# A decoder layer on one core: cross attention's outputs turned in 32x32 blocks on VectorE, its steps dealt out anew, and three shared groups in source order behind it

## The chip, the core and the metric

The kernel runs on 1 core of a Trainium2 chip. The metric is device time in microseconds (us), with the median of several runs. Engines are named as in the profile: PE is TensorE's matmul side and PEld its weight loads, DVE is VectorE, ACT is ScalarE, POOL is GpSimd, SP is SyncE, which here only issues DMAs.

## What is computed

One decoder layer over x of 32 batches x 128 tokens x 512 columns, in float32. Three parts follow one another, each on the layer-normalised sum so far and added to it:

```python
x1 = x + self_attention(layernorm(x))        # differential, 16 heads, causal
x2 = x1 + cross_attention(layernorm(x1), c)  # 8 heads of 16 channels
h3 = layernorm(x2)
out = x2 + shared_mlp(h3) + sum(w_k * expert_k(h3) for k in top6)
```

Cross attention works on each batch as a matrix of 128 channels (partitions) by 512 positions. Queries and keys get a rotary turn, a head's softmax runs over all 512 key positions, and a 128x128 matrix `Wo` leads out. The router takes sigmoid scores of 32 experts in four groups, keeps two groups and picks six experts per token. `shared_mlp` is `down(silu(gate) * up)` with 704 hidden columns over every token. An expert is the same with 352, on the tokens that chose it.

## The kernel before

The program is a list of stages on one core. PSUM is one ring of four tiles of two banks each (`Common.banks`): every user of PSUM takes the next tile and waits until its former user is done with it.

*Cross attention* (about 865 to 2058 us) is written as a hand-made software pipeline, `CrossAttention.advance`. One step is one (batch, side, chunk of 128 queries, pair of heads); 16 steps make a batch and are called a period. In step n the kernel issues

- `maxima` of step n: two matmuls (L621) give scores into a PSUM tile, and one VectorE reduce (L625) takes the row maxima, which frees the tile;
- `exponentials` of step n - 11: two matmuls (L644) on scores less maxima, then one ScalarE exponential (L648);
- in the steps that hold one, a `weigh`, in two halves ahead of and behind these (L659): the weighted values and, by a column of ones, the sums of the weights, 128 x 512 in one bank for each side of a batch;
- whatever `plan` has put down for this step: `sooner` calls ahead of maxima, `later` calls behind exponentials.

`plan` gives each operation of a batch its step by a number written out by hand: the projections, rotations (L590 to L598, VectorE and GpSimd), values, turning the maxima, and behind the weighing `divide` (L667), `turn_out` (L685), `leave` (L694), `measure_out`, `normalize_out`, `hand_over`, `router`, and then the routing: `groups` (L880), `choose` (L904), `take` (L923), `count` (L935), `slots_of`, and six `enter` scatters to a table in DRAM (L957). On PE, VectorE, ScalarE and GpSimd the queue order is the source order (`manual_schedule`). Each engine runs its queue in order, so the plan decides what waits behind what.

Divide and turn before: `weigh` copies its result from PSUM to SBUF on ScalarE (L665). `divide` turns it by eight PE transposes (L674), takes the reciprocal of the sums (L677) and multiplies (L680, twice 128x256) out of PSUM. `turn_out` turns it back by four PE transposes (L83) and a ScalarE copy (L688). `leave` (L697) multiplies by `Wo` and adds x1.

*Behind it*, the shared MLP works in eight groups of 4 batches, `Shared.group`: gate and up in five full chunks (L1126), the ends (L1140), a VectorE multiply by the silu of ScalarE (L1132), then down (L1158 and L1164) for two pairs of batches. Each group loads its tokens (`s_hT`). Two groups come early, behind cross attention: the first with pieces of the routing that are left over (`between`, six calls of `cross.rest(16)`, then `routing.tiles`, which finds out which expert each tile of 128 tokens has), the second beside the start of the experts. Here the scheduler, not the source, orders the instructions. The constructor of `Experts` fetches the tables (GpSimd gathers), turns them on PE (L1224, L1234) and computes places; `begin` starts gathers of tokens (L1310) and the weights' DMAs.

*The experts* (2212 to about 3748) run 208 tiles of 128 tokens in source order: gate and up (L1335), down (L1371), and a scatter-add into `sum_d` (L1376). *The tail* is the six other shared groups, whose sums are written to the output; two DMAs copy the finished early batches.

## Time and profile before

| what | us |
|---|---|
| median of 3 runs (lowest to highest) | 4100.53 (4096.46 to 4104.73) |
| the profiled execution, its own time | 4099.66 |
| its span, first to last instruction | 4098.0 |
| mean granted TensorE clock | 0.992 |
| cross attention, one period | 37.14 |
| end of cross attention to the experts' first matmul | 153.6 |
| one shared group in the tail | 57.46 |

The groups of instructions that matter here, from 1000 to 1900 us of the span, in the form line, engine, operation, operands, count, then busy us, mean ns, and the idle time of the engine just ahead of them:

```profile
L621 PE MATMUL ps<-xk,xq 32*128 32x512 f32 x1550 | 428.4, 633 | 0.0
L644 PE MATMUL ps<-xqn,xk 32*128 32x512 f32 x1550 | 418.0, 638 | 0.0
L659 PE MATMUL ps<-xp,v 128*32 128x512 f32 x1552 | 186.6, 598 | 0.0
...
L674 PE MATMUL ps<-ident,xu 128*128 128x128 f32 x192 | 26.2, 279 | 0.0
```

```profile
L625 DVE TENSOR_REDUCE nm<-ps 128x2 f32<-128x1024 f32 x388 | 473.2, 1225 | 149.3 <-PE ps L621 105.5 <-PE ps L644 40.7
```

L621 and L644 use other row groups of the array (32 of the 128 rows) and run side by side, so their busy times overlap, and busy PE is not PE at its peak. The reduces alone fill 473 of 900 us on VectorE.

### The profile page before, as it was taken

What the parts mean: (1) busy time and instruction counts of PE and PEld (TensorE: products, weight loads), DVE (VectorE), ACT (ScalarE), POOL (GpSimd) and SP (SyncE); (2) the same over time, 40 slices, a digit from 0 to 9 for tenths busy, and PEclk for the clock granted to TensorE, in tenths of its full rate; (3) what the DMA queues carried; (4) which work ended last, traced back from release to release, by engine and by line L of the source; (5) the groups of instructions that cost most, each with busy time, mean ns of one, the idle gap of its engine ahead of it and who ended that gap; (6) DMA issues with size and microseconds to landing.
All of it is one profiled execution on the core that took longest, in us unless ns stands there. A gap on an engine that the chain in (4) does not pass through costs nothing. (4 is left out here: it accounts for less than half of the span.)

```text
span 4098.0 us, 59001 instructions
## 1 busy us (share of the span) xinstructions
PE 3979.2 (97%) x20404; PEld 2081.9 (51%) x20404; DVE 2192.4 (54%) x3461; ACT 1245.6 (30%) x1791; POOL 2241.5 (55%) x2420
## 2 busy tenths in 40 slices
PE   7999999989999999999979999999999999999999
PEld 5666666533344444434335555555555555554444
DVE  5777777777888888888722333333333333332111
ACT  3333333235555555555510111111111111111000
POOL 3444444443555555555444777777777777772000
PEclk9999999999999999999999999999999999999999
DMA  3111110021111111111134777686777776774110
GB/s 105 32 32 31 32 32 27 32 80 38 46 45 40 45 45 45 42 42 45 32 125 117 173 171 195 139 198 155 175 158 174 167 182 155 179 179 115 52 62 31
DMA packets 282785, 386.24 MB, mean 94 GB/s; under 512 B 147792, under 2 KB 175056, under 8 KB 282448
## 3 DMA queue, kind: packets, MB, share of 16 engines
q0 software_dynamic: 62912, 109.85, 15.0%
q1 hardware_dynamic: 77680, 186.52, 14.0%
q10 hardware_dynamic: 141888, 86.01, 7.6%
q8 instruction: 165, 2.70, 0.3%
q14 instruction: 140, 1.15, 0.1%
HBM read 616.47 MB, written 142.02 MB: 185 GB/s over the span
## 5 line engine op out<-in xcount | busy, mean ns | idle before, releaser
L1310 POOL DMA_INDIRECT e_xr<-h_d,e_run_of x832 | 849.4, 1021 | 296.3 <-issue 246.8
L625 DVE TENSOR_REDUCE nm<-ps 128x2 f32<-128x1024 f32 x512 | 623.2, 1224 | 199.6 <-PE ps L621 131.4
L648 ACT ACTIVATE xp<-ps 128x1024 f32<-128x1024 f32 x512 | 516.8, 1023 | 432.0 <-PE ps L644 430.3
L1340 DVE TENSOR_TENSOR e_gu<-e_act,ps 128x352 f32<-128x352 f32 x208 | 108.4, 521 | 956.4 <-ACT e_act L1339 956.4
L1371 PE MATMUL ps<-wd,e_guT 128*128 128x512 f32 (+1 forms) x1248 | 571.7, 594 | 2.2 <-issue 2.1
L621 PE MATMUL ps<-xk,xq 32*128 32x512 f32 x2048 | 564.3, 635 | 6.7 <-DVE xres L403 4.3
L644 PE MATMUL ps<-xqn,xk 32*128 32x512 f32 x2048 | 548.1, 638 | 0.6 <-DVE xqn L633 0.6
L1335 PE MATMUL ps<-wg,e_xT 128*128 128x352 f32 x1664 | 527.7, 459 | 4.2 <-DMA wg<-in_L_ffn_w_gate_dram 3.4
L1335 PE MATMUL ps<-wu,e_xT 128*128 128x352 f32 x1664 | 527.1, 460 | 2.0 <-DMA wu<-in_L_ffn_w_up_dram 1.9
L1335 PEld LDWEIGHTS ps<-wg,e_xT 128*128 128x128 f32 x1664 | 314.8, 189 | 238.3 <-issue 103.4
L1335 PEld LDWEIGHTS ps<-wu,e_xT 128*128 128x128 f32 x1664 | 316.4, 190 | 179.7 <-DMA wu<-in_L_ffn_w_up_dram 3.7
L1376 POOL DMA_INDIRECT sum_d<-e_y,e_into x208 | 338.3, 1627 | 116.7 <-issue 65.0
L1339 ACT ACTIVATE e_act<-ps 128x352 f32<-128x352 f32 x208 | 96.3, 463 | 892.8 <-PE ps L1335 818.4
L1371 PEld LDWEIGHTS ps<-wd,e_guT 128*128 128x128 f32 (+1 forms) x1248 | 238.0, 191 | 247.5 <-issue 204.1
L1375 ACT ACTIVATE e_y<-ps,e_weight 128x512 f32<-128x512 f32 x208 | 142.9, 687 | 421.6 <-PE ps L1371 407.2
L621 PEld LDWEIGHTS ps<-xk,xq 32*128 32x128 f32 x2048 | 158.6, 183 | 220.6 <-ACT xp L648 100.4
L957 POOL DMA_INDIRECT table_d<-entry,at x192 | 196.6, 1024 | 108.7 <-DMA table_d<-entry,at 55.0
L1361 DVE STREAM_TRANSPOSE e_guT<-e_gr 96x384 f32<-96x384 f32 (+1 forms) x416 | 230.3, 554 | 37.9 <-DMA e_gr<-e_gu_d 30.6
L659 PE MATMUL ps<-xp,v 128*32 128x512 f32 x2048 | 247.1, 598 | 3.0 <-ACT xp L648 2.6
L1322 DVE STREAM_TRANSPOSE e_xT<-e_xr 128x512 f32<-128x512 f32 x208 | 226.7, 1090 | 6.4 <-DMA e_xr<-h_d,e_run_of 6.4
L239 POOL TENSOR_SCALAR k<-kz,a_keep,a_extra 128x256 f32<-128x256 f32 x128 | 69.8, 555 | 252.4 <-ACT kz L238 252.4
L644 PEld LDWEIGHTS ps<-xqn,xk 32*128 32x128 f32 x2048 | 152.8, 183 | 37.6 <-DVE nm L625 25.6
(265 smaller groups left out, 5071.9 us busy)
## 6 DMA issues: line engine op xcount, KB each, us to landing
wg<-in_L_ffn_w_gate_dram SPq DMA_DIRECT2D x208, 704.0 KB
wu<-in_L_ffn_w_up_dram SPq DMA_DIRECT2D x208, 704.0 KB
wd<-in_L_ffn_w_down_dram SPq DMA_DIRECT2D x208, 576.0 KB
e_gu_d<-e_gu ACTq DMA_DIRECT2D x208, 192.0 KB
e_gr<-e_gu_d ACTq DMA_DIRECT2D x208, 192.0 KB
wd<-in_L_ffn_w_down_dram SPq DMA_DIRECT2D x208, 128.0 KB
e_xr<-h_d,e_run_of POOLq DMA_INDIRECT x832
xin<-in_x_dram SPq DMA_DIRECT2D x32, 256.0 KB
```

The lines of the kernel that those rows point to most:

```text
L621: self.nc.tensor.matmul(sc[:, i, :], q[rows, ts(c, P)], k[rows, :], start=True, stop=True)
L625: self.nc.vector.tensor_reduce(at[:, self.ROW[side], 2 * pair : 2 * pair + 2], sc, AX.X, ALU.max, negate=True)
L644: self.nc.tensor.matmul(sc[:, i, :], k[rows, ts(c, P)], q[rows, :], start=True, stop=True)
L648: self.nc.scalar.activation(e, sc, AF.Exp)
L659: self.nc.tensor.matmul(po[b, side][ts(j, 32), :], self.v2[b % 2][:, c, 2 * j + side, :], es[j // 2][:, j % 2, :], start=c == 0, stop=c == ...
L957: self.nc.gpsimd.indirect_dma_start(out=self.table_ds[k % 2][:, :], out_offset=bass.IndirectOffsetOnAxis(ap=self.at[b][:, k : k + 1], axis=0),
L1310: self.cm.nc.gpsimd.indirect_dma_start(out=xr[:, t, :], out_offset=None, in_=self.h3_d.rearrange("t (q f) -> (t q) f", q=self.Q), in_offse ...
L1322: self.cm.nc.vector.transpose(xT.rearrange("p c (t i) -> p c t i", t=self.Q), self.xr.pop(i).rearrange("p t (j c) -> p c t j", c=EC),)
L1335: nc.tensor.matmul(pgu[:, half, 0:M], t[:, c, :], w[:, c, :], start=c == 0, stop=c == EC - 1)
L1361: self.cm.nc.vector.transpose(t[rows, 0:n, :].rearrange("p c (t i) -> p c t i", t=self.Q), g[rows, :, 0 : 32 * n].rearrange("p t (j c) -> ...
L1371: nc.tensor.matmul(py, t[:n, c, :], self.wd[s][:n, c, :], start=c == 0, stop=c == len(M_CHUNKS) - 1)
L1376: nc.gpsimd.indirect_dma_start(out=self.sum_d[:, :], out_offset=bass.IndirectOffsetOnAxis(ap=self.into[:, i : i + 1], axis=0), in_=y[:, :] ...
```

## The change

- `weigh`: each side's result is turned in 32x32 blocks by a VectorE `transpose` from PSUM straight to SBUF, in place of ScalarE's copy. Both sides go into one tile `xu` of one buffer.
- `divide`: no PE transposes. One reciprocal and one multiply of 128x512 work on `xu` in SBUF.
- `turn_out`: one VectorE `transpose` of 128x512, SBUF to SBUF, in place of four PE transposes and a copy.
- `plan`: `measure` one step earlier, `measure_out` and `normalize_out` two earlier, `sigmoid` split off from `groups` (steps 43 and 46 in place of 45 for both), `choose` and `take` two later, `count` one later, `slots_of` and the scatters two later. At step 480 the tokens of the first shared group are loaded.
- Behind cross attention: three early groups in place of two, in source order on PE, VectorE, ScalarE and GpSimd. The first two carry the rest of the routing in 33 pieces of two steps and `tiles`; the third carries the experts' table work, cut into `fetch`, `arrange`, `turn_tables`, `places` and `first_tokens`, with fixed places. A group's `sum_d` rows are loaded at its start. The tail has five groups, and the last copies cover 12 batches.

```diff
         if half:
-            self.out[b, side] = self.p2.tile([P, E], F32, name="xu")
-            self.nc.scalar.copy(self.out[b, side], po.pop((b, side)))
+            if side == 0:
+                self.out[b] = self.p2.tile([P, 2, E // 32, 32], F32, name="xu", bufs=1)
+            self.nc.vector.transpose(
+                self.out[b][:, side].rearrange("p k r -> p (k r)"), po.pop((b, side))
+            )
 
     def divide(self, b):
 
-        nc, TC, Q, C, out = self.nc, self.TC, self.Q, self.C, self.out
-        tr = self.cm.banks()
-        for side in range(2):
-            u = out.pop((b, side))
-            for c in range(TC):
-                nc.tensor.transpose(tr[:, side, ts(c, P)], u[:, ts(c, P)], self.cm.ident)
-        tr = tr.rearrange("p s (x r) -> p s x r", r=2 * C)
-        rs = self.p2.tile([P, 2, TC * Q], F32, name="xrs")
-        nc.vector.reciprocal(rs, tr[:, :, :, C])
-        out[b] = self.p2.tile([P, TC * Q, 2, C], F32, name="xo")
-        for side in range(2):
-            nc.vector.tensor_tensor(
-                out[b][:, :, side, :], tr[:, side, :, 0:C],
-                rs[:, side].unsqueeze(2).broadcast_to([P, TC * Q, C]), ALU.mult,
-            )
+        nc, C = self.nc, self.C
+        u, n = self.out.pop(b), E // 32
+        rs = self.p2.tile([P, 2, n], F32, name="xrs")
+        nc.vector.reciprocal(rs, u[:, :, :, C])
+        self.out[b] = self.p2.tile([P, n, 2, C], F32, name="xo")
+        nc.vector.tensor_tensor(
+            self.out[b].rearrange("p k s c -> p s k c"), u[:, :, :, 0:C],
+            rs.unsqueeze(3).broadcast_to([P, 2, n, C]), ALU.mult,
+        )
 
     def turn_out(self, b):
-        tr = self.cm.turn4(self.out.pop(b).rearrange("p x s c -> p (x s c)"))
-        self.out[b] = self.p2.tile([P, self.TC, P], F32, name="xoT")
-        self.nc.scalar.copy(self.out[b], tr)
+        o = self.out.pop(b)
+        self.out[b] = self.p2.tile([P, E], F32, name="xoT")
+        self.nc.vector.transpose(self.out[b], o.rearrange("p k s c -> p (k s c)"))
...
-            sooner.put(at + 29, self.measure_out, b)
-            later.put(at + 31, self.normalize_out, b)
+            sooner.put(at + 27, self.measure_out, b)
+            later.put(at + 29, self.normalize_out, b)
             later.put(at + 38, self.hand_over, b)
             later.put(at + 40, self.router, b)
-            later.put(at + 45, routing.groups, b)
-            sooner.put(at + 53, routing.choose, b)
-            later.put(at + 53, routing.take, b)
-            later.put(at + 55, routing.count, b)
-            sooner.put(at + 61, routing.slots_of, b)
+            later.put(at + 43, routing.sigmoid, b)
+            later.put(at + 46, routing.groups, b)
+            sooner.put(at + 55, routing.choose, b)
+            later.put(at + 55, routing.take, b)
+            later.put(at + 56, routing.count, b)
+            sooner.put(at + 63, routing.slots_of, b)
             for k in range(TOPK):
-                later.put(at + 63 + 5 * k // 2, routing.enter, b, k)
+                later.put(at + 65 + 5 * k // 2, routing.enter, b, k)
         later.put(20, load_shared)
+        later.put(2 * S * (self.B - 2), load_tokens)
         for b in range(self.B):
-            sooner.put(2 * S * b - 11, self.measure, b)
+            sooner.put(2 * S * b - 12, self.measure, b)
...
-        todo = [lambda: cross.rest(16)] * 6 + [
+        todo = [lambda: cross.rest(2)] * 33 + [
             lambda: routing.tiles(eid, fresh, rows, used, usual),
             lambda: nc.sync.dma_start(out=sum_d[T : T + P, :], in_=rest),
         ]
...
-        EARLY = 2
-        shared.group(0, False, between)
+        EARLY = 3
+        with tc.manual_schedule(engines=in_order):
+            for g in range(EARLY - 1):
+                shared.group(g, False, between)
+            while todo:
+                between()
+    e_ctx = ctx.enter_context(ExitStack())
+    with tc.manual_schedule(engines=in_order):
+        experts = Experts(
+            cm, e_ctx, table_ds, h3_d, sum_d, w_gate, w_up, w_down, eid, fresh, rows, n_tiles
+        )
+
+        shared.load_rows(EARLY - 1)
+        experts.begin(0, usual)
+        experts.fetch()
+        nothing = lambda: None
+        todo += [nothing] * 3 + [
+            lambda: experts.arrange(0),
+            lambda: experts.arrange(1),
+            nothing,
+            experts.turn_tables,
+            experts.places,
+            experts.first_tokens,
+        ]
+        shared.group(EARLY - 1, False, between)
         while todo:
             between()
-    e_ctx = ctx.enter_context(ExitStack())
-    experts = Experts(
-        cm, e_ctx, table_ds, h3_d, sum_d, w_gate, w_up, w_down, eid, fresh, rows, n_tiles
-    )
-    experts.begin(0, usual)
-    for g in range(1, EARLY):
-        shared.group(g, False)
     experts.run()
```

More of the change, by code (lines that the diff above doesn't have):

```diff
@@ L697, in leave @@
         self.nc.tensor.matmul(
-            py, self.wT["o"], self.out.pop(b).rearrange("p t x -> p (t x)"), start=True, stop=True
+            py, self.wT["o"], self.out.pop(b), start=True, stop=True
         )
@@ L727, in router, with plan @@
         self.routing.scores(b, pl)
-    def plan(self, load_shared):
+    def plan(self, load_shared, load_tokens):
         S, later, sooner, routing = self.S, self.later, self.sooner, self.routing
@@ L878, in scores, with sigmoid @@
         nc.scalar.activation(s, s, AF.Exp)
-    def groups(self, b):
-        nc = self.nc
-        s = self.score.pop(b)
+    def sigmoid(self, b):
+        nc, s = self.nc, self.score[b]
         nc.vector.tensor_scalar(s, s, 1.0, None, ALU.add)
@@ L889, in groups @@
         )
+    def groups(self, b):
+        nc, s, best = self.nc, self.score.pop(b), self.best[b % 2]
         top = self.small("g_top", [P, 8])
@@ L1098, with __init__, use @@
     G = 4
-    def __init__(self, cm, pool, w, h3T_d, sum_d, out):
-        self.cm, self.pool, self.w, self.h3T_d, self.sum_d, self.out = cm, pool, w, h3T_d, sum_d, out
+    def __init__(self, cm, h_pool, h3T_d, sum_d, out):
+        self.cm, self.h_pool, self.h3T_d, self.sum_d, self.out = cm, h_pool, h3T_d, sum_d, out
         self.NB = h3T_d.shape[0]
-        self.hTs = {}
+        self.hTs, self.x2s = {}, {}
+    def use(self, pool, w):
+        self.pool, self.w = pool, w
     def load(self, g):
@@ L1107, in load @@
         if g * G < self.NB and g not in self.hTs:
-            self.hTs[g] = self.pool.tile([P, G, EC, P], F32, name="s_hT", bufs=2)
+            self.hTs[g] = self.h_pool.tile([P, G, EC, P], F32, name="s_hT")
             self.cm.nc.sync.dma_start(
@@ L1111, in load, with rows_of, load_rows @@
             )
+    def rows_of(self, g, pair):
+        b = g * self.G + 2 * pair
+        return self.sum_d[ts(b // 2, 2 * P), :].rearrange("(b p) e -> p b e", p=P)
+    def load_rows(self, g):
+        if g not in self.x2s:
+            self.x2s[g] = []
+            for pair in range(self.G // 2):
+                x2 = self.pool.tile([P, 2, E], F32, name="s_x2", bufs=2)
+                self.cm.nc.sync.dma_start(out=x2, in_=self.rows_of(g, pair))
+                self.x2s[g].append(x2)
     def group(self, g, final, between=lambda: None):
@@ L1118, in group @@
         self.load(g)
+        self.load_rows(g)
         self.load(g + 1)
@@ L1129, in group @@
                     )
+                if i == 0:
+                    between()
             act = pool.tile([P, G, P], F32, name="s_act", bufs=2)
@@ L1151, in group @@
             b = g * G + 2 * pair
-            rows = self.sum_d[ts(b // 2, 2 * P), :].rearrange("(b p) e -> p b e", p=P)
-            x2 = pool.tile([P, 2, E], F32, name="s_x2", bufs=2)
-            nc.sync.dma_start(out=x2, in_=rows)
+            x2 = self.x2s[g][pair]
             py = cm.banks()
@@ L1161, in group @@
                     )
+                between()
             for i in range(2):
@@ L1168, in group @@
             nc.vector.tensor_tensor(x2, x2, py, ALU.add)
-            to = self.out[b : b + 2].rearrange("b p e -> p b e") if final else rows
+            to = (
+                self.out[b : b + 2].rearrange("b p e -> p b e") if final else self.rows_of(g, pair)
+            )
             nc.sync.dma_start(out=to, in_=x2)
-        between()
 class Experts:
@@ L1203, in __init__, with fetch @@
         T = h3_d.shape[0]
-        self.T = T
-        NT = rows.shape[1]
-        entry = cm.banks().rearrange("p o (j t) -> p o j t", j=EC)
-        parts = cm.banks().rearrange("p o (t j x) -> p (o t) j x", t=2, j=2)
-        for j in range(NT):
-            got = [
-                self.p2.tile([P, E], F32, name="e_y")[:, 0 : 2 * P].rearrange("p (s o) -> p s o", o=2)
-                for i in range(len(table_ds))
+        self.T, self.cp, self.rows, self.table_ds = T, cp, rows, table_ds
+        self.NT = rows.shape[1]
+        self.wg = [cp.tile([P, EC, M], F32, name=f"wg{s}") for s in range(SETS)]
+        self.wu = [cp.tile([P, EC, M], F32, name=f"wu{s}") for s in range(SETS)]
+        self.wd = [cp.tile([P, len(M_CHUNKS), E], F32, name=f"wd{s}") for s in range(SETS)]
+        self.gu_s = cp.tile([P, self.Q * self.RUN], F32, name="e_gu")
+        self.row_i = cp.tile([P, 2], I32, name="e_row_i")
+        self.row = cp.tile([P, 2], F32, name="e_row")
+        self.last, self.expert = None, {}
+        self.got, self.spread = {}, {}
+        self.xr, self.xT, self.gu, self.gr, self.guT = {}, {}, {}, {}, {}
+    def fetch(self):
+        nc = self.cm.nc
+        for j in range(self.NT):
+            self.got[j] = [
+                self.p2.tile([P, E], F32, name=("e_y", "e_xT")[j % 2])[:, 0 : 2 * P].rearrange(
+                    "p (s o) -> p s o", o=2
+                )
+                for i in range(len(self.table_ds))
             ]
-            for t, table_d in zip(got, table_ds):
+            for t, table_d in zip(self.got[j], self.table_ds):
                 nc.gpsimd.indirect_dma_start(
@@ L1218, in __init__ @@
                     in_=table_d.rearrange("(n s) o -> n (s o)", s=P),
-                    in_offset=bass.IndirectOffsetOnAxis(ap=rows[:, j : j + 1], axis=0),
+                    in_offset=bass.IndirectOffsetOnAxis(ap=self.rows[:, j : j + 1], axis=0),
                     bounds_check=table_d.shape[0] // P - 1,
                 )
-            nc.vector.tensor_tensor(got[0], got[0], got[1], ALU.add)
-            for o in range(2):
-                nc.tensor.transpose(entry[:, o, j, :], got[0][:, :, o], cm.ident)
@@ L1226, in __init__ @@
-            runs = self.p2.tile([P, self.Q, self.Q, 32], F32, name="e_xr", bufs=3)
-            slots = got[0][:, :, 0].rearrange("p (b t a) -> p t a b", b=self.Q, t=self.Q)
-            for t in range(self.Q):
-                nc.vector.tensor_copy(
-                    runs[:, t].rearrange("p q (a b) -> p q a b", b=self.Q),
-                    slots[:, t].unsqueeze(1).broadcast_to([P, self.Q, 32 // self.Q, self.Q]),
-                )
+        nc.gpsimd.memset(self.gu_s, 0.0)
+        nc.gpsimd.iota(self.row_i, pattern=[[0, 2]], base=self.T + 1, channel_multiplier=1)
@@ new lines, in arrange @@
+    def arrange(self, j):
+        nc = self.cm.nc
+        got = self.got[j]
+        nc.vector.tensor_tensor(got[0], got[0], got[1], ALU.add)
+        runs = self.spread[j] = self.p2.tile([P, self.Q, self.Q, 32], F32, name="e_xr", bufs=3)
+        slots = got[0][:, :, 0].rearrange("p (b t a) -> p t a b", b=self.Q, t=self.Q)
+        for t in range(self.Q):
+            nc.vector.tensor_copy(
+                runs[:, t].rearrange("p q (a b) -> p q a b", b=self.Q),
+                slots[:, t].unsqueeze(1).broadcast_to([P, self.Q, 32 // self.Q, self.Q]),
+            )
@@ L1233, in __init__, with turn_tables @@
+    def turn_tables(self):
+        nc, cm = self.cm.nc, self.cm
+        self.entry_ps = cm.banks().rearrange("p o (j t) -> p o j t", j=EC)
+        self.parts_ps = cm.banks().rearrange("p o (t j x) -> p (o t) j x", t=2, j=2)
+        for j in range(self.NT):
+            got, runs = self.got.pop(j), self.spread.pop(j)
+            for o in range(2):
+                nc.tensor.transpose(self.entry_ps[:, o, j, :], got[0][:, :, o], cm.ident)
             for t in range(self.Q):
                 nc.tensor.transpose(
-                    parts[:, t, j, :], runs[:, t].rearrange("p q i -> p (q i)"), cm.ident
+                    self.parts_ps[:, t, j, :], runs[:, t].rearrange("p q i -> p (q i)"), cm.ident
@@ L1236, in __init__, with places @@
                 )
-        entry = entry.rearrange("p o j t -> p o (j t)")[:, :, 0:n_tiles]
+    def places(self):
+        nc, cp, T, n_tiles = self.cm.nc, self.cp, self.T, self.n_tiles
+        entry = self.entry_ps.rearrange("p o j t -> p o (j t)")[:, :, 0:n_tiles]
         self.weight = cp.tile([P, n_tiles], F32, name="e_weight")
         nc.vector.tensor_copy(self.weight, entry[:, 1, :])
-        row_i = cp.tile([P, 2], I32, name="e_row_i")
-        nc.gpsimd.iota(row_i, pattern=[[0, 2]], base=T + 1, channel_multiplier=1)
+        row_i, row = self.row_i, self.row
@@ L1243, in __init__ @@
         nc.vector.tensor_scalar(row_i[:, 1:2], row_i[:, 1:2], -T - 1, None, ALU.add)
         nc.vector.tensor_scalar(row_i[:, 1:2], row_i[:, 1:2], 5, None, ALU.logical_shift_right)
-        row = cp.tile([P, 2], F32, name="e_row")
         nc.vector.tensor_copy(row, row_i)
+        self.run_of = cp.tile([P, self.Q, self.NT * P], I32, name="e_run_of")
+        nc.vector.tensor_scalar(
+            self.run_of, self.parts_ps.rearrange("p t j x -> p t (j x)"), float(self.Q),
+            float(-self.Q), ALU.mult, ALU.add,
+        )
@@ L1247, in __init__ @@
+        nc.vector.tensor_scalar(self.run_of, self.run_of, 0.0, row[:, 1:2], ALU.max, ALU.add)
         none = cp.tile([P, n_tiles], F32, name="e_none")
@@ L1250, in __init__ @@
         nc.vector.scalar_tensor_tensor(self.into, entry[:, 0, :], -1.0, none, ALU.add, ALU.add)
-        self.run_of = cp.tile([P, self.Q, NT * P], I32, name="e_run_of")
-        nc.vector.tensor_scalar(
-            self.run_of, parts.rearrange("p t j x -> p t (j x)"), float(self.Q), float(-self.Q),
-            ALU.mult, ALU.add,
-        )
-        nc.vector.tensor_scalar(self.run_of, self.run_of, 0.0, row[:, 1:2], ALU.max, ALU.add)
-        self.wg = [cp.tile([P, EC, M], F32, name=f"wg{s}") for s in range(SETS)]
-        self.wu = [cp.tile([P, EC, M], F32, name=f"wu{s}") for s in range(SETS)]
-        self.wd = [cp.tile([P, len(M_CHUNKS), E], F32, name=f"wd{s}") for s in range(SETS)]
-        self.gu_s = cp.tile([P, self.Q * self.RUN], F32, name="e_gu")
-        nc.gpsimd.memset(self.gu_s, 0.0)
-        self.last, self.expert = None, {}
-        self.xr, self.xT, self.gu, self.gr, self.guT = {}, {}, {}, {}, {}
     def weights_in(self, i):
@@ L1387, in begin @@
         self.first, self.end, self.last = first, end, None
-        for i in range(first, first + 3):
-            self.tokens(i)
         for i in range(first, first + SETS):
@@ L1392, in begin, with first_tokens @@
             self.weights_out(i)
+    def first_tokens(self):
+        for i in range(self.first, self.first + 3):
+            self.tokens(i)
     def run(self):
@@ L1454, in decoder_kernel @@
         cross = CrossAttention(cm, x_w, x1_d, x2_d, h3_d, h3T_d, ctx_in, routing)
-        cross.plan(lambda: s_w.load())
+        cross.plan(lambda: s_w.load(), lambda: shared.load(0))
         x_ctx = ExitStack()
@@ L1480, in decoder_kernel @@
         s_w = SharedWeights(cm, s_w_pool, sw_gate, sw_up, sw_down)
+        s_h_pool = ctx.enter_context(tc.tile_pool(name="s_h", bufs=2, reuse_waits="tile"))
+        shared = Shared(cm, s_h_pool, h3T_d, sum_d, out)
         p2 = ctx.enter_context(tc.tile_pool(name="x_p2", bufs=2, reuse_waits="tile"))
@@ L1484, in decoder_kernel @@
         s_pool = ctx.enter_context(tc.tile_pool(name="s_p", bufs=1, reuse_waits="tile"))
-        shared = Shared(cm, s_pool, s_w, h3T_d, sum_d, out)
-        todo = [lambda: cross.rest(16)] * 6 + [
+        shared.use(s_pool, s_w)
+        en = mybir.EngineType
+        in_order = {en.PE, en.DVE, en.Activation, en.Pool}
+        todo = [lambda: cross.rest(2)] * 33 + [
             lambda: routing.tiles(eid, fresh, rows, used, usual),
@@ L1495, in between @@
                 todo.pop(0)()
-        EARLY = 2
-        shared.group(0, False, between)
+        EARLY = 3
[3 more added lines that the diff above has]
+            while todo:
+                between()
+    e_ctx = ctx.enter_context(ExitStack())
+    with tc.manual_schedule(engines=in_order):
+        experts = Experts(
+            cm, e_ctx, table_ds, h3_d, sum_d, w_gate, w_up, w_down, eid, fresh, rows, n_tiles
+        )
+        shared.load_rows(EARLY - 1)
[11 more added lines that the diff above has]
+        shared.group(EARLY - 1, False, between)
         while todo:
             between()
-    e_ctx = ctx.enter_context(ExitStack())
-    experts = Experts(
-        cm, e_ctx, table_ds, h3_d, sum_d, w_gate, w_up, w_down, eid, fresh, rows, n_tiles
-    )
-    experts.begin(0, usual)
-    for g in range(1, EARLY):
-        shared.group(g, False)
     experts.run()
@@ L1513, in decoder_kernel @@
         experts.begin(usual, n_tiles)
+        experts.first_tokens()
         experts.run()
```

## The prediction, made before the result

> **What bounds the kernel now.** I read the page's busy shares and slices first, then the busy time of each engine by stage, then the order of events on PE and VectorE in one cross attention period, then PE's row through the transition.

> ```profile
> PE 3979.2 (97%) x20404; PEld 2081.9 (51%) x20404; DVE 2192.4 (54%) x3461; ACT 1245.6 (30%) x1791; POOL 2241.5 (55%) x2420
> ...
> PE   7999999989999999999979999999999999999999
> PEld 5666666533344444434335555555555555554444
> DVE  5777777777888888888722333333333333332111
> ```

> PE is busy nearly everywhere, VectorE is at 8 tenths in the slices of cross attention and low behind them. The slice in which PE dips to 7 is the transition to the experts. By stage (columns: window, length, then PE, PEld, DVE, ACT, POOL busy, clock, DMA):

> ```profile
> 1000.00:1900.00 900.00, 884.67 (x5860) 363.46 (x5862) 728.06 (x1191) 529.57 (x653) 503.69 (x720) 1.00 0.14 44
> ...
> 2058.30:2211.90 153.60, 131.30 (x350) 62.28 (x350) 34.36 (x103) 17.40 (x26) 54.78 (x74) 0.93 0.40 127
> ```

> Cross attention looks bound by PE (98%), yet this hides a wait. One period (one batch, 16 steps) takes 37.14 us: the first matmul of L580 for x-rows comes at 1525.15 and again at 1562.29. PE's pieces laid end to end make about 33.7: 16 steps of 1.07, four weigh halves of 1.86, and the projections, turns, divide, leave, hand-over, count and router. In a step the maxima matmuls (L621) and the exponentials' (L644) run side by side, and when one of the pair is held back PE still counts as busy. What holds them shows at the divide:

> ```profile
> 1515.15 1.09 PE L674 MATMUL ps<-ident,xu 128*128 128x128 f32 x8
> ...
> 1517.57 0.63 PE L83 MATMUL ps<-ident,xo 128*128 128x128 f32 x4 [0.19 <-DVE xo L680]
> 1518.12 0.70 PE L621 MATMUL ps<-xk,xq 32*128 32x512 f32 x2
> 1518.63 0.70 PE L644 MATMUL ps<-xqn,xk 32*128 32x512 f32 x2
> ```

> ```profile
> 1514.97 1.23 DVE L625 TENSOR_REDUCE nm<-ps 128x2 f32<-128x1024 f32 x1 [0.93 <-PE ps L621]
> 1516.28 0.36 DVE L677 RECIPROCAL xrs<-ps 128x32 f32<-128x32 f32 x1
> 1516.67 0.75 DVE L680 TENSOR_TENSOR xo<-ps,xrs 128x256 f32<-128x256 f32 x2
> 1517.34 1.23 DVE L625 TENSOR_REDUCE nm<-ps 128x2 f32<-128x1024 f32 x1
> ```

> The reduce that began at 1517.34 ends at 1518.57 and L644 starts at 1518.63: the exponentials wait for the PSUM tile (a ring of four) that VectorE's reduce frees, not for PE. The loop is: maxima start, +1.17 reduce starts, +1.23 ends, +0.05 exponentials start, 2.45 us in all, against 1.07 for a step on PE alone. So cross attention is bound by the queue order of VectorE as much as by PE. I rebuilt a period from this rule and the queue orders, and it gave the starts of before to 0.05 us; I use the same walk for after.

> **The change in cross attention.** Per batch PE loses 8 transposes of L674 (1.02 us) and 4 of L83 (0.55), with 0.19 of idle before them: 1.76. ScalarE loses two copies of 0.585 (L665) and one of 0.580 (L688): 1.75. VectorE keeps the reciprocal (0.36), trades two multiplies (0.75 together) for one of 512 elements, and gains three block transposes. The nearest rows (min/median/max ns):

> ```profile
> L386 DVE STREAM_TRANSPOSE anT<-an x32: 694/698/711, 90.2 to 869.8; 128x512 f32<-128x512 f32 x32
> L352 DVE TENSOR_TENSOR o<-u,rs x64: 668/693/1528, 75.4 to 859.9; 128x512 f32<-128x512 f32 x64
> L928 DVE TENSOR_TENSOR hits<-number,picked x32: 346/1334/1368, 1010.4 to 2101.0; 128x192 f32<-128x192 f32 x32
> ```

> From PSUM L339 turns 128x768 in 974 ns; between 0.70 (as L386, and 974 scaled by size is 0.65) and 0.98 I take 0.70. VectorE per batch: 3 x 0.70 + 0.36 + 0.68 - 1.11 = +2.0, on 30.1 now (728.06/900 of 37.14).

> [...] The trace agrees for L928: 0.35 alone, 1.33 usually, as at 1530.38 to 1531.73, where GpSimd's L592 ran until 1531.50. If the divide behaves as alone it costs 0.68[...]. By the new queue order GpSimd has only the groups' small operations then (0.19 to 0.71), so I take 0.68 and keep 1.9 for the range. [...]

> Walking the new order through the loop, in three stretches that change (the rest of the period stays):

> - From step 15's maxima to the end of the k projection (L580): 12.42 before (1513.79 to 1526.21). Transposes and two PSUM tiles are gone, but reduce, reciprocal, multiply, reduce, turn, reduce now stand in one chain on VectorE: from step 15's maxima 1.17 + 1.14 + 0.39 + 0.60 + 1.14 + 0.61 + 1.23 + 0.05 = 6.33 to step 2's exponentials (pitches, slightly under durations). Result 11.94: -0.48 where PE alone would give -1.76.
> - From the weigh of step 5 to the router's end: 10.95 before (1526.21 to 1537.16). `choose` and `take` stand at step 7 now, `count` at 8; count's matmul (L940) waits for `taken` (L933) behind two reduces. Reduce 6 ends at 7.18, choose 0.72, reduce 7 to 9.04, L928 0.36 and L933 0.49: taken at 9.83, while PE is done at 9.15. Result 11.45: +0.50. I take L928 at 0.36, since the rotation's GpSimd work, which blocked it at step 5, is over by then; blocked, it adds 1.0. If PE has other work in hand, this stretch gives 0.
> - From the q projection to the weigh of step 13: 1.32 before. The row statistics of the output (1.01 on VectorE) now stand before reduce 11 and so before the exponentials: 1.95, +0.63. Unless the order has slack, then 0.

> Moved steps bring their DMAs and GpSimd calls along: six scatters per batch two steps later, the h3 stores as before, and one 1 MB load of tokens at step 480 on SP, where the queue is nearly empty (DMA share 0.14). I cost these at nothing; the cover is GpSimd at 56% here. The sum is +0.6 us a period, with bounds -0.1 (second and third stretch hidden) and +1.9 (divide blocked). Some 28 full periods: +17. The end of the stage gains 2.57 of wait (below): cross attention +15.

> **The transition.** From the end of cross attention to the experts it takes 153.6 now, with two shared groups. PE waits:

> ```profile
> 2057.21 1.05 PE L659 MATMUL ps<-xp,v 128*32 128x512 f32 x4 [2.57 <-ACT xp L648]
> 2062.50 5.53 PE L1126 MATMUL ps<-s_hT,sg 128*128 128x512 f32 x8 [4.23 <-DMA s_hT<-h3T_d]
> ...
> 2130.54 7.38 PE L1158 MATMUL ps<-sd,s_gu 128*128 128x512 f32 x12 [7.25 <-DVE s_gu L1132]
> ```

> With the smaller ones between them (1.33, 0.68, 0.31, 2.80, 3.34, 2.40) they make 24.9, and the mean clock of this window was 0.93. A group takes 57.46 in the tail, where nothing disturbs it (34.53 + 3.45 + 8.58 + 1.06 + 8.78 + 1.06). After: three groups, 172.4; the rest of routing and leave (1.05, two hand-overs, counts and routers of 0.59, 0.56 and 1.0) 5.4; turning the tables (12 transposes) 2; stalls. Source order removes the first wait (exponentials stand ahead of the last h3 on ScalarE), the early load the second, and the 7.25 with 2.40, since the table fetch (POOL) starts a group ahead of its use. New waits: the last down matmul of the third group needs VectorE's L1132 result, behind which `turn_in` waits for the tokens' gathers, eight of about 1.4 us from 34 us into the group, so at 47 against a need at 49: 0 to 3. Routing chains on VectorE (2.80 and 3.34 before) may stall once more under in-order queues. I take 5 for all; between 0 and the old 20. Sum 185, which is +31; the tail has one group less, -57.5. Together -26 (-33 to -10). The 2.1 MB weight sets start a group (over 50 us) ahead of the experts, so these start undelayed. The earlier early group adds 4 batches to the final copies, beside other groups' PE work: nothing. Experts themselves: unchanged.

> **Sum.** +15 - 26 = -11 on the profiled run's 4099.66 (span 4098.0), or 4088.6; its run lies 0.87 under the median of 4100.53, so I say 4089.

> **Rivals and chances.** A measurement of this kernel can tell about 0.2% (8 us) from no change.
> - Forecast, order of VectorE eats what PE gains, transition pays: 4089 (4075 to 4092), 0.45.
> - PE's relief is realised: the stretches 2 and 3 have slack or transposes are cheaper. Period -0.8 to -1.76 (the 1.57 removed plus idle): -22 to -50, with -26: 4026 to 4050. For it: PE at 98%; against: the 2.45 loop in every step with an extra operation. Part of it (period about -0.1) gives about 4070. Together 0.20.
> - No change to be told: period +0.8 to +1.1 or transition -10, 4092 to 4108: 0.22.
> - [...] The divide (or L928) falls beside a 1.27 us GpSimd rotation in each batch, period +1.9, 28 x 1.9 = +53 - 2.6 - 26 = +24: 4125. It decides from 28p = 28.6 + 8, a period of +1.3. For it: L928 at 1.33 now; against: GpSimd's rotation lies elsewhere in the new order. 0.13.
> - That the reordering does not do what it says, and the transition keeps its old waits of 20: +46 - 57.5 + 15 = +4, or 4104; it is in the third case.

> Faster 0.65, no change 0.22, slower 0.13. Range 4058 to 4112.

> **What would show it.** Period near 37.7 by the start of successive k projections; L940 idle behind L933; the divide's multiply at 0.65 to 0.7 [...]; the new turn from PSUM at 0.70; VectorE 85% in the middle of cross attention; transition 180 to 190 with no wait on `s_hT`; five groups of 57.5 in the tail. I am wrong if the period is under 37 (PE relieved after all) or the transition is over 200.

## The result, and the profile after

The changed kernel takes 4078.57 us (median of 4 runs, 4075.13 to 4080.70), the kernel before 4101.24 beside it: a ratio of 0.9939, 95% interval 0.9920 to 0.9958. That is 22.7 us less; 11.5 were forecast. The profiled execution took 4079.63 with a span of 4077.9, 20.1 under that of before. Lines have moved: L625 is L627 now, L621 and L644 are L623 and L646, L928 is L933, L1126 is L1149.

By stage, the same columns as ahead of the change (window, length, busy PE, PEld, DVE, ACT, POOL, clock, DMA). The second row is the transition, from its first shared matmul to the first of the experts:

```profile
1000.00:1900.00 900.00, 849.73 (x5513) 326.04 (x5513) 715.94 (x1223) 477.48 (x575) 512.17 (x712) 1.00 0.16 45
2068.70:2248.33 179.63, 179.60 (x486) 84.78 (x482) 45.23 (x137) 19.96 (x31) 59.13 (x85) 1.00 0.36 116
```

PE fell from 98% to 94% busy in cross attention: it lost work and the time did not shrink, so the difference turned into waiting. VectorE was forecast at 85% and is at 80%: 29.9 us a period (715.94 of 900, times 37.55) against 30.0 before. The exchanged operations add the 2.0 us of the forecast, but L933 became 0.99 shorter and the router's `score` (TENSOR_SCALAR) 0.30; the rest was not traced. In the transition PE is busy for 179.60 of 179.63 us, at full clock; before it was 131 of 154, at 0.93.

A period takes 37.55 (k projections, which the forecast's text calls x-rows, at 1536.42 and 1573.97), 0.41 more than before. The queue of VectorE behind step 15 is the chain of the forecast, in the order of the source and start for start:

```profile
1564.27 1.23 DVE L627 TENSOR_REDUCE nm<-ps 128x2 f32<-128x1024 f32 x1 [0.34 <-PE ps L623]
1565.41 0.34 DVE L678 RECIPROCAL xrs<-xu 128x32 f32<-128x32 f32 x1
1565.79 0.69 DVE L680 TENSOR_TENSOR xo<-xu,xrs 128x512 f32<-128x512 f32 x1
1566.40 1.22 DVE L627 TENSOR_REDUCE nm<-ps 128x2 f32<-128x1024 f32 x1
1567.53 0.70 DVE L688 STREAM_TRANSPOSE xoT<-xo 128x512 f32<-128x512 f32 x1
```

and PE stands behind it. The transposes of the maxima in the last row (L83) wait for the reduce of 1566.40, which itself waited for the divide:

```profile
1565.55 0.70 PE L623 MATMUL ps<-xk,xq 32*128 32x512 f32 x2 [0.17 <-DVE nm L627]
...
1567.67 0.66 PE L83 MATMUL ps<-ident,nm 128*128 128x128 f32 x4 [0.84 <-DVE nm L627]
```

The durations of the operations that the forecast bounded (min/median/max ns):

```profile
L680 DVE TENSOR_TENSOR xo<-xu,xrs x32: 691/692/720, 925.5 to 2070.0; 128x512 f32<-128x512 f32 x32
L933 DVE TENSOR_TENSOR hits<-number,picked x32: 347/348/359, 1020.6 to 2153.8; 128x192 f32<-128x192 f32 x32
```

No multiply of the divide was ever held up (720 at most), though GpSimd's L962 runs beside it in 26 of the 32 batches. L933 was held up in most batches before (median 1334): 27 of the 32 start while GpSimd's L592 runs, take 1325 to 1368 ns and end 0.21 to 0.22 us behind it, and the five others take 346 to 359. At its new step it never is (359 at most), with L962 beside it in 27 batches. The turn from PSUM (L668) has a median of 717 ns, against 700 assumed.

Behind cross attention, PE goes from the last weigh to the first shared group without a wait, where it stood for 4.23 us before:

```profile
2065.12 3.64 PE L661 MATMUL ps<-xp,v 128*32 128x512 f32 x32
2068.70 3.70 PE L1149 MATMUL ps<-s_hT,sg 128*128 128x512 f32 x8
```

The 20.1 us of the two spans by stage, from the first matmuls of each:

| stretch | before | after | difference | forecast |
|---|---|---|---|---|
| to the last batch's k projection | 1970.88 | 1987.05 | +16.2 | +17 |
| from there to the end of cross attention | 87.4 | 81.7 | -5.7 | -2.6 |
| end of cross attention to the experts | 153.7 | 179.6 | +26.0 | +31 |
| experts | 1536.0 | 1537.1 | +1.0 | 0 |
| tail | 350.0 | 292.5 | -57.5 | -57.5 |

The first row came out close to its forecast by two errors that offset each other. There are 26 periods of full length, not 28, and each rose by 0.41, not 0.6: 10.7 us in all. Another 5.6 come from the third to the fifth period, in which the pipeline fills (34.63, 34.63 and 36.34 before, 36.83, 37.65 and 36.71 after) and which the forecast did not count; in the third and in the fourth the changed kernel's clock stood at 0.50 for 6.83 us (from 929.63 and from 967.17), that of before in none of the three. The two profiled runs account for 20.1 of the 22.7 us between the medians; the rest lies between executions of one kernel.

### The profile page after: what moved, and what is told of

Its sections match the earlier page's. It is cut to its first block, busy times and chain, and to the rows that moved or that the text cites. A ratio compares the mean times of both kernels' runs of the same rounds, so it can differ in the third digit from the quotient of the medians.

```text
span 4077.9 us, 58248 instructions
## 1 busy us (share of the span) xinstructions
PE 3940.9 (97%) x20020; PEld 2036.1 (50%) x20020; DVE 2197.2 (54%) x3525; ACT 1184.3 (29%) x1695; POOL 2256.2 (55%) x2420
## 3 DMA queue, kind: packets, MB, share of 16 engines
q14 instruction: 139, 1.14, 0.1%
## 5 line engine op out<-in xcount | busy, mean ns | idle before, releaser
L627 DVE TENSOR_REDUCE nm<-ps 128x2 f32<-128x1024 f32 x512 | 622.8, 1218 | 165.5 <-PE ps L646 148.9
L623 PE MATMUL ps<-xk,xq 32*128 32x512 f32 x2048 | 561.1, 632 | 11.8 <-DVE nm L627 7.3
L646 PE MATMUL ps<-xqn,xk 32*128 32x512 f32 x2048 | 513.6, 640 | 1.4 <-DVE xqn L635 0.6
L623 PEld LDWEIGHTS ps<-xk,xq 32*128 32x128 f32 x2048 | 164.5, 185 | 250.1 <-ACT xp L650 99.8
L962 POOL DMA_INDIRECT table_d<-entry,at x192 | 211.2, 1100 | 63.1 <-issue 43.3
L646 PEld LDWEIGHTS ps<-xqn,xk 32*128 32x128 f32 x2048 | 154.7, 184 | 94.2 <-DVE nm L627 73.3
```

The lines of the kernel that those rows point to most:

```text
L623: self.nc.tensor.matmul(sc[:, i, :], q[rows, ts(c, P)], k[rows, :], start=True, stop=True)
L627: self.nc.vector.tensor_reduce(at[:, self.ROW[side], 2 * pair : 2 * pair + 2], sc, AX.X, ALU.max, negate=True)
L646: self.nc.tensor.matmul(sc[:, i, :], k[rows, ts(c, P)], q[rows, :], start=True, stop=True)
L962: self.nc.gpsimd.indirect_dma_start(out=self.table_ds[k % 2][:, :], out_offset=bass.IndirectOffsetOnAxis(ap=self.at[b][:, k : k + 1], axis=0),
```

## The experiments

The theory: a period's length is set by what stands ahead of each reduce in VectorE's queue, since the exponentials wait for the PSUM tile that the reduce frees. PE's work and VectorE's load only set a floor. The rivals: PE's work sets the period; VectorE's load sets it. For the expectations I replayed the queue orders of PE, VectorE, ScalarE and GpSimd by the rule of the forecast, with durations from the two traces. This gives 37.2 for the kernel before (37.14 measured) and 37.55 for the changed one (37.55). "The walk" below is this replay. It was made after the result, so these two agreements are a fit; only its numbers for x1 to x9 are forecasts.

| run | ratio to before, 95% interval | periods, us |
|---|---|---|
| changed kernel | 0.9939 (0.9920 to 0.9958) | 37.55 |
| x1 old steps | 0.9913 (0.9892 to 0.9933) | 37.06 |
| x2 old divide | 0.9996 (0.9987 to 1.0006) | 38.04, each fourth 39.5 |
| x3 transition alone | 0.9933 (0.9910 to 0.9955) | 37.13 |
| x4 cross attention alone | 1.0018 (1.0011 to 1.0026) | 37.55 |
| x5 statistics back | 0.9980 (0.9966 to 0.9995) | 37.1 and 38.07, four near 40 |
| x6 steps dealt out anew | 0.9652 (0.9636 to 0.9668) | 33.36 |
| x7 the same for PE's transposes | 0.9737 (0.9720 to 0.9753) | 34.64 |
| x8 other steps | 0.9680 (0.9664 to 0.9696) | 33.95 |
| x9 divide spread | 0.9936 (0.9916 to 0.9956) | 38.0, 38.0, 36.50 in turn |
| x10 fill at the turn | 0.9943 (0.9924 to 0.9962) | 37.1 and 38.07 |
| x11 two early groups | 1.0000 (0.9987 to 1.0014) | 37.55 |
| x12 fill at count | 0.9862 (0.9842 to 0.9883) | 36.65 |

The kernel before took a median of 4103, 4100, 4112 and 4117 us beside x1 to x4, x5 to x8, x9 to x11 and x12, so across these sets the ratios are compared, and the periods. A difference of some us in time between two runs can come from the experts: their code is the same in all, and in the kept traces they take from 1532.4 (x8) to 1556.8 us (x10).

**x1: the new transposes with the old steps.** The diff puts the steps of before back (`measure_out` 29, `choose` and `take` 53, `count` 55 and so on; `sigmoid` again in `groups`).

> The changed kernel with the steps of before (VectorE's block transposes kept, routing's sigmoid and groups together again). Theory: the period is set by what stands ahead of each reduce in VectorE's queue; walking the order through that rule gives 37.3 us a period (changed kernel: 37.55), so about 6 us less than it, 4072. Rival, the new steps are what makes the transposes bearable (take at step 5 blocked 1.0 us by GpSimd in every batch): period 38.5 or more, 4105. Rival, PE's work sets the period: the steps make no difference, 37.55, 4079.

4068.48 us, period 37.06. The theory holds; the walk was 0.2 too long. The new steps were no cover for the transposes, they cost 0.49 a period. The block of `take`'s first operation that the rival counts on is not there at the old step either (316 ns in the median, 360 at most). Behind the last k projection the new steps do pay: with the old ones the end of cross attention takes 87.5, where the changed kernel takes 81.7, and most of that is a wait for an exponential that the source order did not remove:

```profile
2053.31 1.71 PE L661 MATMUL ps<-xp,v 128*32 128x512 f32 x4 [3.92 <-ACT xp L650]
```

**x2: the old divide with the new steps.** `weigh`, `divide` and `turn_out` of before in the changed kernel.

> The changed kernel with weigh, divide and turn_out of before (PE transposes and ScalarE copies) under the new steps. Theory (order of VectorE's queue): 37.9 a period by the walk, 4088. Rival, PE's work sets the period: 1.76 more each, 39.3, 4128. Rival, VectorE's load sets it: 2.0 less each, 35.5, 4022.

4099.57 us, 12 more than the theory's. The undisturbed period is 38.04, near the walk, and far from both rivals. Each fourth period takes 39.5; why is told with x9. So under the new steps the block transposes gain 0.49 a period (38.04 to 37.55), the forecast's 0.48; under the old ones 0.07 (x3's 37.13 to x1's 37.06). PE lost the same 1.57 us of work in both. Behind the last k projection x2 takes 84.7 to the end of cross attention and 181.6 to the experts, against 81.7 and 179.6.

**x3: the new transition alone.** Cross attention wholly as before, all behind it as changed.

> Cross attention wholly as before, with the new transition (three early groups in source order, tokens loaded at step 480). Theory: the two parts add; period 37.14 as before, so 16 us less than the changed kernel up to the last batch, and some 3 us more behind it, where the divides stand again: 4066. Rival, the transition is as short as it is because cross attention's end is lighter on PE: transition 10 us longer, 4076 or more.

4077.08 us: the rival's number. The period is 37.13, but its transition takes 186.1 against 179.6, and the end of cross attention 6.2 more (87.8 from the last k projection, against 81.7). Much of this is the clock: it stood at 0.50 for 6.8 us in each of the two stretches (0.96 on average from the last k projection to the end of cross attention, 0.98 in the window 2070 to 2240; 1.00 in the changed kernel), which costs some 3.4 us each, half of the 6.8, an estimate. In the transition one wait of 2.28 us shows (L1186, behind `s_gu`), and PE's own transposes add about 1.3. Some 4 us more lie in the experts (1541.3 against 1537.1), whose instructions are the same. So the two parts do not add. What the transposes alone are worth behind the loop is seen better against x2, which has the old divide with the changed kernel's steps and no such fall: 3.1 us at the end of cross attention and 1.9 in the transition.

**x4: the new cross attention alone.** The kernel before with the new `weigh`, `divide`, `turn_out` and steps, the old transition.

> The kernel before with the new cross attention alone (block transposes and new steps; two early groups and the old transition). Theory: period 37.55, 16 us more by the last batch, 6 less at its end: 4111. Rival, PE's relief shows when the transition is left alone: under 4095.

4113.00 us, period 37.55. As expected: cross attention's part of the change is a loss. From the last k projection to the last weigh's end it takes 81.7 like the changed kernel, without the wait for an exponential, though the transition is the old one.

**x5: the statistics of the output back.** Of the new steps, only `measure_out` and `normalize_out` go back:

```diff
-            sooner.put(at + 27, self.measure_out, b)
-            later.put(at + 29, self.normalize_out, b)
+            sooner.put(at + 29, self.measure_out, b)
+            later.put(at + 31, self.normalize_out, b)
```

> The changed kernel with only measure_out and normalize_out at their old steps (29 and 31). Theory: the walk gave this move 0.63 us in its stretch; by the whole walk the period falls from 37.55 to 37.2, and the time by 11 to 4068. Rival, the stretch's loss is taken up elsewhere by slack: 37.55, 4079.

4089.35 us (4082.74 to 4102.09), a miss. The best periods are 37.09, as the theory has it (37.2), but others take 38.07 and four of them 39.8 to 40.7. In the slow ones the granted clock is 0.96 or less (0.87 in the worst), in the fast ones 1.00. A second mechanism is at work, see x9 to x12.

**x6: every step dealt out by the walk.** The changed kernel with these steps, and nothing else touched:

```diff
-            later.put(at - 12, self.project, b, "k")
-            sooner.put(at - 11, self.rotate, b, "k")
-            later.put(at - 8, self.normalize, b)
-            later.put(at - 5, self.project, b, "q")
+            later.put(at - 10, self.project, b, "k")
+            sooner.put(at - 7, self.rotate, b, "k")
+            later.put(at - 7, self.normalize, b)
+            later.put(at - 4, self.project, b, "q")
...
-            later.put(at - 2, self.values, b)
+            later.put(at + 1, self.values, b)
...
-            later.put(at + 15, self.divide, b)
-            later.put(at + 16, self.turn_out, b)
-            later.put(at + 18, self.leave, b)
-            sooner.put(at + 27, self.measure_out, b)
-            later.put(at + 29, self.normalize_out, b)
+            later.put(at + 17, self.divide, b)
+            later.put(at + 22, self.turn_out, b)
+            later.put(at + 25, self.leave, b)
+            sooner.put(at + 29, self.measure_out, b)
+            later.put(at + 34, self.normalize_out, b)
...
-            later.put(at + 43, routing.sigmoid, b)
-            later.put(at + 46, routing.groups, b)
-            sooner.put(at + 55, routing.choose, b)
-            later.put(at + 55, routing.take, b)
+            later.put(at + 44, routing.sigmoid, b)
+            later.put(at + 45, routing.groups, b)
+            sooner.put(at + 53, routing.choose, b)
+            later.put(at + 54, routing.take, b)
```

(`slots_of` and the scatters come three steps earlier, `measure` one later.)

> The changed kernel with VectorE's block transposes and every step dealt out by walking orders through the rule until no reduce is held up (among others divide 17, turn_out 22, leave 25, normalize_out 34, choose 53, take 54). Nothing is left out. Theory (order of VectorE's queue, not its load): 33.7 us a period, close to PE's 32.1, 28 x 3.9 = 108 less, 3970. Rival, VectorE's load bounds it (32.1 busy of 37.55): not under 36, 4035. Rival, the order doesn't matter, PE's speed does: 37.55, 4079.

3956.79 us, the fastest version here, 3.5% under the kernel before. The period is 33.36, and VectorE is busier than in the changed kernel:

```profile
1000.00:1800.00 800.00, 762.62 (x5520) 289.64 (x5520) 719.79 (x1224) 478.61 (x576) 506.78 (x718) 1.00 0.17 51
```

90% of VectorE (719.79 of 800), against 80% (715.94 of 900) in the changed kernel, with the same instructions. So its load was not the bound (nor was it 32.1 us a period, as expected: 29.9 in the changed kernel, 30.0 here). The order was.

**x7: the same search with PE's transposes.** The divide of before in the changed kernel, steps dealt out for it (`divide` 17, `turn_out` 19, `leave` 24, `choose` 51, `take` 53 and others).

> PE transposes and ScalarE copies of before in the changed kernel, with steps dealt out for them in the same way. Theory: 34.9 a period (PE's work 33.7), 4004: the order is worth more than the block transposes, which are then worth PE's 1.2 a period. Rival, the block transposes are what makes a short period possible: not under 36.5, 4050.

3994.33 us, period 34.64. A good order is worth 2.5 us a period (from 37.14) without any block transpose. With a good order for each, the block transposes gain 1.28 of PE's 1.57.

**x8: other steps that the walk rates as high.** `divide` 16, `turn_out` 20, `leave` 25, `router` 35, `sigmoid` 40 and others.

> As x6_dealt_anew with other steps that the walk finds as good (divide 16, turn_out 20, leave 25, router 35, sigmoid 40). Theory: 33.6, 3970, within 10 us of x6. If x6 is good and this is not, the walk fits one order by luck.

3966.80 us, period 33.95. This is 10.0 us over x6, at the edge of what was expected. The walk does not fit one order by luck; it was off by 0.3 us in each of the two, but in opposite directions, so it cannot rank orders that lie this close.

**x9: the divide alone spread out.** In place of 15, 16 and 18:

```diff
-            later.put(at + 15, self.divide, b)
-            later.put(at + 16, self.turn_out, b)
-            later.put(at + 18, self.leave, b)
+            later.put(at + 17, self.divide, b)
+            later.put(at + 19, self.turn_out, b)
+            later.put(at + 21, self.leave, b)
```

> The changed kernel with only divide, turn_out and leave moved: steps 17, 19 and 21 in place of 15, 16 and 18, so that reciprocal and multiply, the turn and the add no longer stand behind one another in VectorE's queue. Theory (the chain on VectorE behind step 15 is what eats PE's gain): 36.5 a period by the walk, 29 less than the changed kernel, 4049. Rival (the stretch's gain is given back in the other two): 37.55, 4079.

A miss: a ratio of 0.9936 and no gain, though VectorE's chain is gone: three reduces now run without a pause ahead of the divide.

```profile
1363.59 3.68 DVE L627 TENSOR_REDUCE nm<-ps 128x2 f32<-128x1024 f32 x3 [0.34 <-PE ps L623]
1367.19 0.34 DVE L678 RECIPROCAL xrs<-xu 128x32 f32<-128x32 f32 x1
1367.57 0.69 DVE L680 TENSOR_TENSOR xo<-xu,xrs 128x512 f32<-128x512 f32 x1
```

Three periods in a row show where the gain went (the clock is the third column from the right):

```profile
1333.19:1371.18 37.99, 36.86 (x232) 14.86 (x231) 29.97 (x52) 20.15 (x24) 21.29 (x30) 0.96 0.14 42
1371.18:1409.19 38.01, 36.86 (x231) 14.54 (x230) 29.97 (x52) 20.15 (x24) 21.30 (x30) 0.96 0.14 43
1409.19:1445.69 36.50, 35.66 (x232) 13.81 (x230) 29.89 (x52) 20.06 (x24) 21.30 (x30) 1.00 0.15 45
```

The third is the walk's 36.5 to the hundredth; the other two lose 1.5 us to the clock. In steps of one us (length, busy PE, clock, DMA):

```profile
1347.00:1348.00 1.00, 1.00 (x9) 0.73 0.00 0
1348.00:1349.00 1.00, 1.00 (x6) 0.50 0.00 0
1349.00:1350.00 1.00, 1.00 (x6) 0.50 0.00 0
1350.00:1351.00 1.00, 1.00 (x12) 0.56 0.06 16
```

The clock falls to 0.50 for some 3.4 us while PE is busy throughout (a pair of L623's matmuls takes 1.06 to 1.22 us there, 0.59 to 0.70 at the clock of 1.00); just ahead, PE had stood idle for 0.66 us in front of count's matmuls, and the router's short ones followed:

```profile
1345.18 0.38 PE L945 MATMUL ps<-taken,before 128*128 128x32 f32 x2 [0.66 <-PE ps L623]
```

The falls of x2 and most of x5's begin at this place of the period too, 12 to 14 us behind the k projection.

**x10: a fill ahead of the turn of the maxima, on x5.**

```diff
+        ps = self.cm.banks()
+        if side:
+            self.nc.tensor.matmul(
+                ps[:, 1, 0:384], self.cm.ident, self.cos["k"][:, 0:384], start=True, stop=True
+            )
...
```

> x5_stats_back with one idle matmul of 128x384 per batch, whose result nobody reads, ahead of the second turn of the maxima, where PE stood idle for 0.84 us and where the granted clock fell to 0.50 behind it. It adds work to PE. Theory (x5 lost its gain to the clock: PE looked idle too long there): granted clock back to 0.99, 37.1 in every period, 4067, although PE does more. Rival (the clock falls for another reason, such as the phase of the period, or x5's loss isn't the clock's): 4085 or more.

A ratio of 0.9943 beside x5's 0.9980: the two intervals overlap, and by the ratio neither the theory's number (0.992) nor the rival's (0.996 or more) came. The long periods of 39.8 to 40.7, whose clock fell behind this turn, are not seen any more; those of 38.07, whose clock falls at the other place, stay. The fill did not take the place of the wait: it stands behind the same 0.84 us itself, since it needs the same PSUM tile (1185.35, 0.84 behind `nm`). Inconclusive.

**x11: two early groups in source order.** `EARLY = 2`, nothing else.

> The changed kernel with two early groups in place of three, still in source order, so that half of the rest of routing stands uncovered between the groups. Theory (the transition gained by the third group being cover): the uncovered rest of routing and tiles costs 10 to 20 us, 4093. Rival (it gained by the order alone, the group only moved from the tail): 4079.

A ratio of 1.0000, about 25 us over the changed kernel, where the theory had 14. The transition takes 148.7 with two groups, of which 114.9 are the groups; the changed kernel's 179.6 hold 172.4 of groups. What stands uncovered is PE waiting, 18.4 us in all, most of it for the last batch's routing and for the tables, and the clock is 0.92 over the stretch, against 1.00:

```profile
2136.80 0.61 PE L945 MATMUL ps<-taken,before 128*128 128x32 f32 x2 [10.54 <-DVE taken L938]
2171.33 0.70 PE L1285 MATMUL ps<-ident,e_xT 128*128 128x128 f32 x2 [5.80 <-DVE e_xT L1268]
```

So the source order alone gains nothing between the groups and the experts (148.7 against 149.4 before); the third group, which moves work that must be done anyway into that place, makes it 30.9 longer and the tail 57.4 shorter. The waits in front of the groups are another matter: the 4.23 us for `s_hT` are gone here as well.

**x12: a fill ahead of count, on x9.**

```diff
+        ps = self.cm.banks()
+        nc.tensor.matmul(
+            ps[:, 1, :], self.before, self.cross.cos["k"], start=True, stop=True
+        )
...
```

> x9_divide_spread with one idle matmul of 128x512 per batch, whose result nobody reads, ahead of count's matmuls, where PE stands idle for 0.66 us and behind which the granted clock falls to 0.50 for 3.4 us in two of three periods of x9. It adds 1.0 us of work to PE in each batch. Theory (the clock falls because PE did too little in the few us before): no fall any more, 36.5 to 36.9 in every period where x9 has 36.5, 38.0, 38.0; some 20 us less than x9, ratio to before 0.989. Rival (another cause): periods of 38.0 remain, ratio 0.994 or more.

A ratio of 0.9862 beside x9's 0.9936, and every period takes 36.65. PE has 1 us more to do in each batch, and 0.9 us less pass on average (37.53 to 36.65). No wait ahead of count is left, and the clock no longer falls, here in the two windows that were x9's slow periods:

```profile
1333.19:1371.18 37.99, 37.81 (x241) 14.50 (x237) 31.23 (x54) 21.20 (x26) 21.30 (x30) 1.00 0.14 42
1371.18:1409.19 38.01, 37.83 (x242) 14.48 (x244) 31.20 (x56) 21.39 (x26) 21.54 (x31) 1.00 0.14 43
```

## Why the prediction was right, and by how much it missed

The direction and the mechanism were right; the time lay in the range, but the gain was twice the forecast's. By its steps:

- **The 2.45 us loop of reduce and exponentials**, held up by VectorE's queue, as the bound of cross attention: that the order bounds is shown by x6, where the same instructions in another order take 33.36 us a period; that it does so by this loop rests on the walk, which foretold the undisturbed periods of x1 to x9 to 0.4 us.
- **The three stretches.** From step 15 to the k projection: 11.93 measured, 11.94 forecast. From the weigh of step 5 to the router's end: 11.31 (1537.47 to 1548.78), 11.45 forecast; count waited 0.66 for `taken`. From the q projection to the weigh of step 13: 1.96, 1.95 forecast. The two stretches that I held for unchanged shrank by 0.1 together. The period rose by 0.41, with 0.6 forecast; the transposes' part by itself is -0.49 (x2), -0.48 forecast. The sum to the last k projection, 16.2 with 17 forecast, is in part luck, as told above.
- **The slower rival, a divide held up by GpSimd**: it did not come. The multiply stayed at 0.69. The 1.9 kept for it in the range was an estimate: the multiply's 0.68 and the 1.27 of an operation like L592, behind whose end L928 ended before. L933 was relieved of its 1 us, but not by its new step alone (x1 has it at 316 ns at the old one); what the relief was worth by itself was not measured.
- **The end of cross attention**, the first mis-sized term: -5.7 in place of -2.6. Only the exponentials' wait (2.57) was counted. The PE work of the two divides that lie here, 1.57 each, was put at nothing. x2, with the old divide and the same steps, takes 3.1 us longer here: 0.5 up to the second count, as in any period, and 2.6 behind it, where the last reduces run out. The wait itself was credited to the source order. With the old steps that order removes it under the old divide (x3 has none) but not under the block transposes (x1 has 3.92), and with the new steps it is gone without that order (x4); why was not traced.
- **The stalls of the transition**, the second: 5 were put in, none came (179.60 of 179.63 us busy). The waits of the routing's chain and of the tables lay under the three groups; x11 shows them as 10.54 and 5.80 us when one group is missing. I took the cover at less than it was. Part of it is the lighter divide: with the old one, x2's transition takes 1.9 us more.
- **The rival "PE's relief is realised"** failed for this plan, under which 0.49 of 1.57 us comes through, and for the old one (0.07). With a good order for each divide 1.28 comes through (x7 to x6). The larger gain, 2.5 us a period with the old divide (37.14 to 34.64, x7), is the order itself, which none of my cases held.
- **The clock** stood in no case. In the full periods of the changed kernel it did not fall (1.00 from 974 to 1986 us), while x2, x5 and x9, a few steps away, lost 0.3 to 1.0 us a period to it on average. That the change escaped this is luck too (see the last section).

## What to carry to other kernels

An engine that is busy 98% of the time can be waiting all the same, if two of its instructions run side by side (in the trace of before L644 from 1518.63 for 0.70 us and L621 from 1518.66 for 0.59); lay the pieces end to end and look for the difference (33.7 of 37.14 us here). When work moves to another engine of a hand-made pipeline, its in-order queue has to be dealt out again around the one operation that everything waits for: here the order was worth 2.5 us of 37 a period with the old divide and 4.2 with the new one, the moved work itself between 0.07 and 1.28, depending on the order. Work that must be done anyway is worth most where a chain of small dependent operations would stand bare.

## What the runs showed of the hardware

PE's granted clock fell to 0.50 in a stage where PE was 97% busy (36.86 of 37.99 us in x9): for 3.41 us at a time behind waits of 0.66 us and a few short matmuls (x2, x5, x9, x10), and for 6.83 behind waits of 0.84 to 0.94 in x5. One idle matmul of 128x512 in the wait of 0.66 us prevented it in x12, whose clock is 1.00 from 900 to 1900 us.
